# Cross-attention with layer norm: two key blocks evacuated ahead of a cast, the last eight pairs reordered

## The chip, the cores and the metric

The kernel runs on one core of a Trainium2 chip. The metric is the device time of one execution in microseconds (us), lower is better. The engines are TensorE (PE, its weight loads PEld), VectorE (DVE), ScalarE (ACT), GpSimd (POOL) and SyncE (SP, which only issues DMAs). Each engine works through its own instructions in program order.

## The reference

```python
# x (4, 2048, 512), context (4, 77, 512), mask (4, 2048, 77); 16 heads of 32; all float32
qs  = heads(x @ wq); ks = heads(ctx @ wk); vs = heads(ctx @ wv)
scores = einsum('bhqd,bhkd->bhqk', qs, ks) / sqrt(32)
scores = where(mask, -inf, scores)
attn   = einsum('bhqk,bhkd->bhqd', softmax(scores), vs)
out    = concat_heads(attn) @ wo + x
mu, var = mean(out), mean((out - mu)**2)          # over the 512 columns
result = (out - mu) / sqrt(var + 1e-5) * gamma + beta
```

## The kernel before

The 8192 rows are 64 tiles of 128 rows; two tiles make a block (32 blocks, called pairs), four tiles a group (16 groups, 512 rows). The context is so short that the keys (kct) and values (vsb) of all four batches stay in SBUF. Projections are done in split precision: an operand is cast to fp32r (the high part, by ScalarE) and the rest is kept as a low part (by GpSimd or VectorE), and three matmuls of 512 columns for each of 4 chunks, 12 in all, make one product.

The work is not scheduled by a compiler: the string ORDER lists it word by word, and each engine gets its part of the words in that order. A word is a letter with a number (a tile t, a pair b, or group times four plus part) and perhaps a part. The words used below:

- TensorE: S t scores of a tile (four PSUM banks sc, one for each place of a head in its group); Q one of four query projections of a group; V b product of probabilities and values of a pair (banks pa); W t the same for one tile, in the last pair; O t output projection (bank po); X t adds the residual x into po as a matmul by the identity, ahead of O t.
- VectorE: T t.n row maxima of four heads, with the mask (reads sc, writes pbuf); r reciprocal of the sums; t t transposes the probabilities (pbuf to B); q evacuates Q; b (and d in the last pair) the low part AL of the attention result; + residual into SBUF, $ residual in PSUM; s statistics (bn_stats, bn_aggr); y and z centring and finishing (subtract the mean and multiply by gamma; multiply by the inverse deviation and add beta).
- ScalarE: e t.n exponentials of four heads with their sums; a (c in the last pair) the high part AH of the attention result; i the cast of a half group of inputs (xth); k and % scale and shift a tile by its statistics; K evacuates a key block from PSUM into kct, in two instructions (J does so on VectorE).
- GpSimd: n normalises a tile's probabilities (h and m do so by halves for tile 63); j the low part of an input half (xtl); v, u, @ inverse deviations; f multiplies by gamma and adds beta.
- DMA: P b.n and U t.n move the transposed probabilities, in twelve pieces of a pair, from B to PT, on SyncE's queue (s), GpSimd's (g) or ScalarE's (a); x loads a tile for the residual, g a half group of inputs, w stores a tile.

A tile's path is S, T, e, r, n, t, P, V, a and b, O, then + or $, s, and either k with f, % with f, or y with z, then w. In the steady middle each pair of tiles repeats the same order of words. The last eight pairs (tiles 48 to 63) are written out in an order of their own, and in them the statistics are taken tile by tile.

Which of its buffers a tile takes is set by the strings SLOTS: "mm" gives the PSUM bank (0 to 7) for each product in the order of the program. A product waits until the reader of its bank's former holder is done. PADS gives the number of NO_OPs that stand between the matmuls of each projection. At the start, the words around the change are:

```python
... K2 A2 H2 J3 p i3 g4 J1 K0 i2 S0 I2 j2 S1 T0.1 ...
"K": lambda k, part: keys_evac(k, nc.scalar), "J": lambda k, part: keys_evac(k, nc.vector),
"i": lambda k, part: cast_xT(k // 2, k % 2 * 2),
```

H2 is a query projection of group 0, I2 its evacuation, S0 and S1 the first scores; i3 and i2 are the casts of group 1, whose inputs lie in stage_a.

Of the kernel before, what the change touches and what calls it, by code (L numbers as in the profile page):

```python
# [121 lines left out]
P24.3s M60.4 P25.11s T53.2 Q57 P25.4s e53.0 q58 P25.5s r52 T53.1 n52 P25.1s e53.2 b23.0 P25.2s T53.3 S54 P25.10s
e53.1 w43 v22 T54.0 Q56 e53.3 T54.1 x48 q57 P25.8s P25.3g q59 k42 P25.6s r53 T54.2 e54.1 n53 V24 b23.1 T54.3 e54.3
q56 x53 S55 f42 t52 a24.1 O46 a24.0 i31 t53 e54.2 b24.1 P26.10g P26.5s X49 i30 P26.6g +46 P25.7s P26.11g b24.0
P25.0s O49 P26.9a j31 T55.0 P25.9s e54.0 T55.3 P26.8s T55.1 w42 k45 T55.2 P26.1s j30 e55.0 S56 s46 r54 T56.1 O47
e55.3 T56.3 n54 s49 e55.2 T56.0 T56.2 S57 e56.0 f45 t54 V25 e55.1 T57.3 +47 O48 e56.2 w45 r55 P26.4g s47 P26.0s n55
a25.0 x55 T57.1 a25.1 P26.2s T57.2 e56.3 x57 Q61 $48 v23 t55 e56.1 u49 y49 P27.4s P26.7a Q63 b25.0 P26.3s e57.3
P27.11g q61 x51 P27.3g T57.0 P27.0s P27.1g e57.0 s48 P27.8g P27.2g r56 S58 b25.1 e57.2 P27.10g z49 n56 Q62 q63 k46
T58.2 k47 T58.1 e57.1 T58.3 f46 T58.0 V26 q62 e58.0 r57 t56 n57 S59 k44 w46 x61 e58.3 Q60 T59.0 P27.6s T59.1 P27.7s
e58.1 @48 T59.3 x50 t57 P27.9s f44 a26.1 P27.5s O50 a26.0 T59.2 e58.2 P28.8s q60 P28.9s b26.1 P28.5s e59.3 P28.6g  # L130
r58 b26.0 x63 S60 n58 $50 P28.3s e59.1 T60.1 O53 w44 T60.0 P28.1s %48 T60.2 x59 e59.2 P28.10g P28.0s t58 P28.2g
P28.11s X51 f47 e59.0 x56 T60.3 S61 +53 e60.0 T61.3 O51 r59 T61.2 n59 e60.1 T61.1 s50 e61.2 V27 T61.0 t59 P28.4g
e60.2 P28.7g f48 S62 s53 P29.8s e61.1 P29.2s T62.0 x58 s51 O52 a27.0 w47 a27.1 y51 w48 e60.3 P29.7g b27.0 P29.9s
u51 b27.1 P29.6s e61.3 y50 V28 P29.10s P29.1g r60 P29.0g z51 P29.11s e61.0 P29.3g T62.3 x54 n60 T62.2 x52 O55 a28.0
x62 T62.1 a28.1 r61 P29.5a b28.0 n61 b28.1 e62.1 t60 S63 e62.2 O57 t61 P29.4g e62.0 u50 T63.0 P30.2s @53 e62.3 +55
P30.6s O56 T63.2 P30.0s P30.5g T63.1 e63.0 P30.10s P30.11g r62 P30.3g s55 P30.8s n62 e63.1 P30.1s $52 X63 w51 T63.3
e63.3 V29 s52 @55 z50 e63.2 t62 @52 X62 P30.9a O54 h63.0 U62.5g U62.2s $56 a29.1 m63.0 a29.0 h63.1 U62.8s s56
P30.7a b29.0 m63.1 P30.4a b29.1 %52 O58 u56 t63 %55 f52 U62.4a $54 U62.3a U63.4s y56 U63.11s V30 $58 U63.0s z56
a30.0 U62.9s U63.10g s58 U62.11a U62.7s U63.7g O59 %53 $57 U62.1s U63.6g a30.1 U63.3g s57 U62.6s U62.10a @58 w52
b30.0 U63.1a U63.2s b30.1 u57 O61 U63.8a y57 f53 U63.5a s54 U62.0a z57 %58 y54 w57 U63.9a O60 $59 f55 +61 s61 s59  # L140
W62 @61 $60 w55 w53 s60 W63 u54 c62 w50 %61 u59 d62 O62 c63 u60 y59 z59 f61 d63 w59 z54 w56 y60 O63 z60 f58 w61 s62
w49 w54 y62 w60 s63 u62 w58 y63 u63 z62 z63 w62 w63
"""

SLOTS = {
    "mm": (
        "7012346570123576402317564023617520135647205130627431726352740136217364514036572140635170625341026713"
        "6427014536270652734107265320146735204167245310762435102367540123765427106345270163205417362045172463"
        "5071243650231764052371642750134627051320645731204657241360752431602357140623751427605341270653201467"
        "3520416724531076243510236754012376542710634527016320541736204517246350712465032634756320417537621047"  # L150
        "2362147310654130761370645732064023706457326475236123073042"
    ),
    "q": "1010101010101010",
    "xth": "010101010101010101",
# [4 lines left out]
    "AH": "1010010101010101010101010101010010",  # L159
    "AL": "1010010101010101010101010101010010",  # L160
    "o": "765401237654231607541237510462375104623751046237510462375104362",
# [17 lines left out]
def xattn_layernorm(  # L179
# [410 lines left out]
    def residual_psum(t):  # L590
        nc.vector.tensor_tensor(pos[t], pos[t], od[t], ALU.add)
# [36 lines left out]
    def moments_one(t):  # L628
# [3 lines left out]
        nc.vector.bn_aggr(mvs[t, 1][:, :2], st)
# [13 lines left out]

    def centre(t):
        o = pos.get(t, od[t])
        nc.vector.scalar_tensor_tensor(o, o, mvs[t, 1][:, 0:1], gam, ALU.subtract, ALU.mult)

    def finish(t):
        nc.vector.scalar_tensor_tensor(od[t], pos.pop(t, od[t]), mvs[t, 1][:, 2:3], bet, ALU.mult, ALU.add)
# [160 lines left out]
```

## Time and profile before

| what | value |
|---|---|
| median of 3 runs | 512.13 us (511.66 to 512.14) |
| the profiled execution's own time | 512.37 us |
| its span, first to last instruction | 510.5 us |
| mean granted TensorE clock | 0.997 |
| instructions in the span | 21819 |
| bytes moved by DMA | 110.95 MB, mean 217 GB/s |

A row of a stretch (A:B) gives its length, then for each engine the busy time with the number of instructions, the granted clock, the busy share of the DMA engines and GB/s. A row of the timeline gives the start, the time taken, engine, line, operation, output<-input and shapes; in brackets stands how long the engine was idle before it and what ended the wait. A row of the chain that ended last gives start, duration, engine, what was made and how many instructions were merged. A row of a group gives the count, the busy time and the mean in ns, then the idle time before. The times of the profile are those of one execution. Matmuls overlap, so the spacing of their starts says more than their listed length.

### The profile page before, as it was taken

The page shows a single profiled execution, that of the slowest core. Times are in us where ns is not written, and L with a number is a line of the kernel's source. Part 1 is how long each engine was busy: PE and PEld are TensorE (multiplying, and loading weights), DVE is VectorE, ACT ScalarE, POOL GpSimd, SP SyncE. Part 2 cuts the span into 40 slices and gives each one's busy share as a digit, 9 for nine tenths or more (in the row PEclk, how much of TensorE's full clock was granted, in tenths as well). Part 3 has the DMA queues.
Part 4 walks back from the last instruction along what each step waited for, and adds up shares of the span by engine and source line. Part 5 has one row for each costly group of instructions (what it writes and reads, how often), then busy time and mean ns, then how long its engine had stood idle before and what let it go on. Part 6 is the DMA issues. An engine that isn't in the chain of part 4 may idle for free.

```text
span 510.5 us, 21819 instructions
## 1 busy us (share of the span) xinstructions
PE 499.6 (98%) x6836; PEld 384.9 (75%) x6836; DVE 470.8 (92%) x2565; ACT 463.4 (91%) x2221; POOL 421.9 (83%) x389
## 2 busy tenths in 40 slices
PE   9999999999999999999999999999999999999994
PEld 7887777777777777777777877777777767776673
DVE  6698999999999999999999999999999899999897
ACT  6599999998999999999999999999999999899720
POOL 3473756899978998989899898888999689999896
PEclk9999999999999999999999999999999999999998
DMA  8947678868877777796768676876777875688655
GB/s 312 390 131 220 170 190 191 248 174 243 248 213 229 217 234 198 223 241 201 236 194 239 199 217 187 245 230 182 216 209 224 233 204 167 178 241 258 175 170 217
DMA packets 59139, 110.95 MB, mean 217 GB/s; under 512 B 9414, under 2 KB 11934, under 8 KB 59030
## 3 DMA queue, kind: packets, MB, share of 16 engines
q1 hardware_dynamic: 55094, 102.09, 68.7%
q0 software_dynamic: 2512, 5.84, 4.1%
q10 hardware_dynamic: 1424, 1.64, 1.2%
q8 instruction: 60, 0.98, 0.9%
q14 instruction: 49, 0.40, 0.3%
HBM read 41.79 MB, written 16.78 MB: 115 GB/s over the span
## 4 chain that ended last, share of the span: by engine, by line
PE 81%; POOL 7%; DMA 5%; DVE 4%; issue 1%; SPq 1%; ACT 0%; DVEq 0%; POOLq 0%; ACTq 0%
PE pq L290 33%; PE po L579 26%; PE sc L414 10%; PE pa L507 9%; DVE B L482 2%; PE pv L341 2%; DMA PT<-B 2%; DMA stage_a<-xT 2%; DMA stage_a<-wk 1%; POOL PT L493 1%; POOL o L621 1%; POOL xtl L273 1%; POOL pbuf L461 1%; POOL o L622 1%; POOL mvt L637 1%
## 5 line engine op out<-in xcount | busy, mean ns | idle before, releaser
L446 ACT ACTIVATE pbuf<-pbuf,nm 128x77 f32<-128x77 f32 x1024 | 352.4, 350 | 4.3 <-DVE nm L431 3.9
L446 ACT ACTIVATION_READ_ACCUMULATOR pbuf<-pbuf,nm 128x1 f32 x1024 | 195.5, 191 | 0.0
L431 DVE CUSTOM_DVE_ANT_0 pbuf<-sc,mb 128x77 f32<-128x77 f32 x1024 | 171.3, 233 | 9.1 <-PE sc L414 5.3
L461 POOL TENSOR_TENSOR pbuf<-pbuf,ri 128x1232 f32<-128x1232 f32 x63 | 142.8, 2267 | 30.4 <-DVE ri L456 28.9
L579 PE MATMUL po<-woh,AH 128*128 128x512 f32 x256 | 102.2, 399 | 1.8 <-DVE nm L431 1.4
L290 PE MATMUL pq<-xth,wqh 128*128 128x512 f32 (+1 forms) x256 | 101.3, 396 | 0.4
L579 PE MATMUL po<-woh,AL 128*128 128x512 f32 x256 | 100.0, 391 | 0.2
L579 PE MATMUL po<-wol,AH 128*128 128x512 f32 x256 | 99.8, 390 | 0.0
L482 DVE STREAM_TRANSPOSE B<-pbuf 128x1280 f32<-128x1280 f32 x64 | 95.9, 1500 | 2.9 <-POOL pbuf L473 1.4
L290 PE MATMUL pq<-xtl,wqh 128*128 128x512 f32 (+1 forms) x256 | 98.1, 383 | 0.0
L290 PE MATMUL pq<-xth,wql 128*128 128x512 f32 (+1 forms) x256 | 98.1, 383 | 0.0
L431 DVE DVE_READ_ACCUMULATOR2_ANT nm<- 128x1 f32 x1024 | 84.5, 83 | 0.0
L273 POOL TENSOR_TENSOR xtl<-xtf,xth 128x1024 fp32r<-128x1024 f32 x28 | 67.3, 2408 | 5.8 <-ACT xth L269 5.7
L622 POOL TENSOR_TENSOR o<-o,bet 128x512 f32<-128x512 f32 x52 | 67.3, 1294 | 4.1
L414 PEld LDWEIGHTS sc<-kct,q 32*64 32x64 f32 x4096 | 51.3, 130 | 23.7 <-issue 9.7
L621 POOL TENSOR_TENSOR o<-o,gam 128x512 f32<-128x512 f32 x52 | 68.4, 1315 | 0.2 <-issue 0.2
L414 PE MATMUL sc<-kct,q 32*64 32x77 f32 x4096 | 60.7, 238 | 0.9 <-ACT kct L326 0.9
L507 PE MATMUL pa<-PT,vsb 96*32 96x256 f32 x992 | 59.7, 382 | 0.0
L579 PEld LDWEIGHTS po<-woh,AH 128*128 128x128 f32 x256 | 48.1, 188 | 14.8 <-PE pa L507 1.0
L290 PEld LDWEIGHTS pq<-xth,wqh 128*128 128x128 f32 x256 | 48.0, 188 | 12.5 <-issue 1.2
L579 PEld LDWEIGHTS po<-woh,AL 128*128 128x128 f32 x256 | 48.0, 188 | 11.5 <-DVE AL L540 1.4
L579 PEld LDWEIGHTS po<-wol,AH 128*128 128x128 f32 x256 | 48.1, 188 | 9.8 <-issue 0.5
(120 smaller groups left out, 640.8 us busy)
## 6 DMA issues: line engine op xcount, KB each, us to landing
PT<-B SPq DMA_DIRECT2D x339, 128.0 KB
xtf<-xT SPq DMA_DIRECT2D x28, 512.0 KB
o<-x SPq DMA_DIRECT2D x56, 256.0 KB
out<-o SPq DMA_DIRECT2D x56, 256.0 KB
PT<-B POOLq DMA_DIRECT2D x26, 128.0 KB, 4.4
stage_a<-wk SPq DMA_DIRECT2D x4, 256.0 KB
stage_b<-wo SPq DMA_DIRECT2D x4, 256.0 KB
stage_a<-xT SPq DMA_DIRECT2D x2, 512.0 KB
```

What stands on the lines that cost most here:

```text
L273: nc.gpsimd.tensor_tensor(l[:, c : c + 2], fx.pop((g, c)), xh[g][:, c : c + 2].bitcast(F32), ALU.subtract)
L290: nc.tensor.matmul(pq, w[:, c, m * P : (m + 1) * P], r[g][:, c, rs], start=(n == 0), stop=(n == 11))
L341: nc.tensor.matmul(pv[: rows.stop - rows.start], ctx_s[c][i][:, rows], v[c], start=(n == 0), stop=(n == 11))
L414: mm = nc.tensor.matmul(sc[j][r0 : r0 + SR, g * NK : (g + 1) * NK], qs[q, g, rs.start + r0 : rs.start + r0 + SR], kct[q, g, t // TPB, keys ...
L431: nc.vector.tensor_tensor_reduce(pb[:, h // 2, (h % 2) * NK : (h % 2 + 1) * NK], scs[t][j][:, g * NK : (g + 1) * NK], mb[:, t % TPB, keys_ ...
L446: nc.scalar.activation(pb[:, h // 2, (h % 2) * NK : (h % 2 + 1) * NK], pb[:, h // 2, (h % 2) * NK : (h % 2 + 1) * NK], AF.Exp, bias=nmax[t ...
L461: nc.gpsimd.tensor_tensor(pv, pv, rv.to_broadcast((P, NP, 2, NK)), ALU.mult)
L482: nc.vector.transpose(bt.rearrange("p c q r -> p q c r"), pbuf[t % NPB].rearrange("p q (c r) -> p q c r", c=5),)
L507: nc.tensor.matmul(pas[b, g // 2][HD * j : HD * (j + 1), (g % 2) * BLK : (g % 2 + 1) * BLK], vsb[:, 2 * b // TPB, h % 2, HD * (h // 2) : H ...
L579: nc.tensor.matmul(pos[t], a[:, c, rs], w[:, c, :], start=(first and c == 0 and n == 0), stop=(c == NC_D - 1 and n == 2),)
L621: nc.gpsimd.tensor_tensor(o, o, gam, ALU.mult)
L622: nc.gpsimd.tensor_tensor(o, o, bet, ALU.add)
```

## The change

1. At the start, K0 is put ahead of the cast i3 (K0 g4 J1 i3 i2 in place of i3 g4 J1 K0 i2).
2. From g27 on, the input loads stand about a pair earlier; the order of the last eight pairs is new, with the PSUM banks that belong to it. The residual of tile 49 is added by VectorE ($49) in place of TensorE (X49); tile 48 is centred and finished by VectorE (u48 y48 z48) in place of ScalarE and GpSimd (@48 %48 f48); for 52 and 58 the residual goes to SBUF (+52, +58) in place of PSUM.
3. For tiles 60 and 62 ScalarE takes the statistics (=60, =62): one pass that sums the tile to minus its mean, and one that sums the squares of the centred values. GpSimd then scales that sum in place of adding epsilon alone.
4. Tile 63 is finished and stored in two halves of 256 columns (>63.0 <63.0 >63.1 <63.1), the first stored by SyncE's queue, the second by ScalarE's.
5. PADS is shifted at a few projections early in the program and around tile 26; there are 1466 NO_OPs in place of 1469. Some of the transposed pieces change their queue.

```diff
-... K2 A2 H2 J3 p i3 g4 J1 K0 i2 S0 I2 j2 S1 T0.1
+... K2 A2 H2 J3 p K0 g4 J1 i3 i2 S0 I2 j2 S1 T0.1
...
-    "i86800000000000000000686c10000cfmmlllllllllmmmmmmmmmmmmmmmmmmkkkkkkkkkkkkkkkkkkkkkkkkkkkkkkkkkjkkk00"
+    "f8680000000000000000000686000cddlmmllllllllmmmmmmmmmmmmmmmmmmmmikkkkkkkkkkkkkkkkkkkkkkkkkkkkkkjkkk00"
...
+    def stats_act(t):
+        mv = mvs[t, 1] = tiny.tile([P, 4], F32, tag="mvt", bufs=64 - LATE, name=f"mvt_{t}")
+        nc.scalar.activation(od[t], pos[t], AF.Copy, scale=-1.0 / D, accum_out=mv[:, 3:4])
+        nc.scalar.activation(od[t], pos[t], AF.Square, bias=mv[:, 3:4], accum_out=mv[:, 1:2])
+        by_act.add(t)
+
     def rsqrt_one(t):
         mv = mvs[t, 1]
-        nc.gpsimd.tensor_tensor(mv[:, 2:3], mv[:, 1:2], eps[:, :1], ALU.add)
+        if t in by_act:
+            nc.gpsimd.tensor_scalar(mv[:, 2:3], mv[:, 1:2], 1.0 / D, EPS, ALU.mult, ALU.add)
+        else:
+            nc.gpsimd.tensor_tensor(mv[:, 2:3], mv[:, 1:2], eps[:, :1], ALU.add)
         nc.gpsimd.tensor_tensor(mv[:, 2:3], mv[:, 2:3], mhalf[:, :1], ALU.pow)
...
     def centre(t):
         o = pos.get(t, od[t])
-        nc.vector.scalar_tensor_tensor(o, o, mvs[t, 1][:, 0:1], gam, ALU.subtract, ALU.mult)
+        m, op = (3, ALU.add) if t in by_act else (0, ALU.subtract)
+        nc.vector.scalar_tensor_tensor(o, o, mvs[t, 1][:, m : m + 1], gam, op, ALU.mult)
...
+    def finish_half(t, i):
+        cols = slice(i * D // 2, (i + 1) * D // 2)
+        nc.vector.scalar_tensor_tensor(
+            od[t][:, cols], pos[t][:, cols], mvs[t, 1][:, 2:3], bet[:, cols], ALU.mult, ALU.add
+        )
+
+    def store_half(t, i):
+        cols = slice(i * D // 2, (i + 1) * D // 2)
+        (nc.sync, nc.scalar)[i].dma_start(out[t * P : (t + 1) * P, cols], od[t][:, cols])
...
+        "=": lambda k, part: stats_act(k), ">": finish_half, "<": store_half,
```

TensorE's words from the scores of tile 52 on, before and after:

```
before: S52 V23 S53 Q59 Q58 Q57 S54 Q56 V24 S55 O46 X49 O49 S56 O47 S57 V25 O48 Q61 Q63 S58 Q62 V26 S59 Q60 O50
        S60 O53 X51 S61 O51 V27 S62 O52 V28 O55 S63 O57 O56 X63 V29 X62 O54 O58 V30 O59 O61 O60 W62 W63 O62 O63
after:  S52 V23 S53 Q56 Q58 S54 O46 Q59 S55 Q57 V24 S56 O47 O49 V25 S57 O48 Q60 Q61 S58 Q63 Q62 S59 V26 O50
        S60 X51 O53 S61 O51 S62 V27 O52 V28 O55 S63 O54 X63 O57 X62 V29 O56 O58 V30 O59 O61 O60 W62 W63 O62 O63
```

More of the change, by code (lines that the diff above doesn't have):

```diff
@@ L109 @@
 T44.0 e44.1 P20.1s T44.2 x40 S45 s36 a19.0 P20.0s e43.1 T44.3 Q48 v18 P20.3s t42 P20.9s P20.11s f34 k37 P20.8s
-T45.0 a19.1 P20.5s Q49 e44.2 T45.2 x43 r43 b19.1 n43 e44.3 b19.0 T45.3 T45.1 O39 e44.0 M48.4 f37 q49 e45.0 t43 O38
-e45.3 q48 P21.7s r44 w34 +39 i26 n44 P21.2s s39 k36 P21.4s S46 +38 e45.2 w37 V20 j26 T46.1 P21.10s T46.0 P21.6s
+T45.0 a19.1 P20.5s Q49 e44.2 T45.2 g27 r43 b19.1 x43 n43 e44.3 b19.0 T45.3 T45.1 O39 e44.0 M48.4 f37 q49 e45.0 t43
+O38 e45.3 q48 P21.7s r44 w34 +39 i26 n44 P21.2s s39 k36 P21.4s S46 +38 e45.2 w37 V20 j26 T46.1 P21.10s T46.0 P21.6s
@@ L122 @@
[L122 to L141, printed above, removed]
@@ L142 @@
-w49 w54 y62 w60 s63 u62 w58 y63 u63 z62 z63 w62 w63
+T51.2 P23.5s r49 g30 b22.1 x49 n49 e50.3 b22.0 T51.3 T51.1 O45 e50.0 q55 f43 t49 e51.0 q54 P24.7s O44 e51.3 r50 w40
++45 n50 P24.4s s45 e51.2 P24.3s P24.9s S52 i29 +44 x63 P24.2g M60.4 P24.11s V23 e51.1 T52.2 P24.1g P24.5s j29 T52.0
+P24.6s e52.2 T52.3 S53 P24.0s t50 x51 e52.3 Q56 P24.8s r51 T52.1 n51 a23.0 T53.0 e52.1 s44 Q58 q56 a23.1 v22 e52.0
+T53.2 b23.0 b23.1 P24.10a t51 S54 k44 e53.0 O46 r52 P25.3g P25.7s T54.1 n52 g31 T53.3 e53.2 P25.6s T53.1 w43 T54.0
@@ new lines @@
+e53.1 Q59 P25.2s T54.3 f44 x60 T54.2 e53.3 P25.11s t52 P25.5s e54.0 P25.9s S55 M56.4 P25.1s r53 +46 Q57 n53 e54.1
+q59 P25.10s T55.0 P25.0s e54.3 T55.2 P25.8s q58 P25.4g V24 e54.2 q57 t53 a24.0 S56 i30 T55.1 P26.10g P26.2s r54
+a24.1 O47 x56 T56.0 j30 e55.2 x57 b24.0 x48 b24.1 P26.0s e55.0 s46 P26.5s T55.3 O49 P26.11g w44 e55.3 T56.3 P26.4g
+P26.3s +47 n54 P26.8s T56.2 e55.1 P26.1s T56.1 V25 $49 e56.0 r55 t54 n55 e56.2 S57 x52 s49 O48 x58 i31 T57.3 u49
+y49 k42 j31 s47 e56.3 T57.0 Q60 T57.2 e57.3 f42 t55 a25.0 P26.7a z49 P27.7s Q61 e56.1 $48 w42 q60 P26.6g w49 T57.1
@@ new lines @@
+e57.2 P27.11g P26.9s s48 P27.1g S58 P27.3g e57.0 q61 x53 P27.2g y48 Q63 P27.4s u48 r56 a25.1 T58.2 n56 k45 T58.3
+e57.1 b25.0 T58.0 Q62 T58.1 e58.0 P27.8g z48 P27.10g r57 w48 b25.1 e58.1 n57 t56 P27.5s S59 P27.6s e58.2 V26 q62
+f45 T59.2 e58.3 t57 O50 a26.0 a26.1 T59.1 P28.11s e59.2 P27.0g T59.0 P28.1s P28.7g q63 P27.9s e59.0 v23 r58 S60
+b26.0 P28.9s T59.3 P28.8s X51 e59.1 n58 b26.1 P28.5s T60.1 O53 x59 T60.0 e59.3 P28.3s T60.2 P28.0s t58 e60.2
+P28.10g x55 P28.2g x61 S61 P28.4g e60.1 +53 P28.6g O51 r59 T60.3 n59 k47 T61.2 e60.3 T61.0 T61.3 f47 S62 T61.1
@@ new lines @@
+e60.0 t59 V27 e61.1 r60 T62.2 e61.3 P29.11s P29.0g T62.3 O52 P29.7g x50 s51 P29.4g P29.8s a27.0 T62.0 P29.3g a27.1
+P29.2s s53 P29.6g e61.0 w45 P29.1g V28 b27.0 P29.10s n60 y51 e61.2 x62 b27.1 T62.1 O55 a28.0 r61 @53 a28.1 $50
+e62.3 +52 n61 b28.1 b28.0 k46 S63 t60 e62.2 x54 f46 O54 e62.1 t61 P29.5a +55 w46 e62.0 T63.1 X63 P30.11g P29.9s
+T63.0 P30.5g O57 P30.6s P30.3g T63.2 e63.1 P30.1s u51 r62 s52 P30.0s n62 e63.2 s50 P30.2s P30.8s X62 T63.3 e63.3
+P30.10s s55 V29 u50 w47 y50 e63.0 @52 z51 @55 z50 w51 O56 a29.0 h63.0 P30.4a $57 m63.0 h63.1 a29.1 b29.0 P30.9a s57
@@ new lines @@
+m63.1 P30.7a b29.1 O58 %55 u57 t62 %53 f55 %52 $56 U62.2s U62.11a V30 $54 U62.1s U62.10a +58 U62.6s U62.3a f53 t63
+U62.4a O59 a30.0 a30.1 s58 U63.4s U63.1a U63.11s b30.0 @58 U62.8a U62.9s b30.1 U62.0a s56 U62.7s O61 U63.9a U62.5g
+y57 U63.10g U63.3a s54 U63.6g U63.0s U63.5a U63.7g U63.2s y54 U63.8a u54 w50 O60 +61 %58 f52 w53 z54 s61 $59 y56
+W62 @61 s59 W63 c62 u56 z57 u59 c63 d62 O62 $60 f58 y59 =60 d63 z59 %61 y60 O63 w59 u60 =62 z56 w58 f61 z60 w57 y62
+w56 w60 s63 w52 w55 u62 y63 w61 u63 z62 w54 w62 >63.0 <63.0 >63.1 <63.1
@@ L158 @@
     "B": "0101011010101010101010101010101010",
[L159 to L161 removed]
+    "AH": "1010010101010101010101010101010101",
+    "AL": "1010010101010101010101010101010101",
+    "o": "765401237654231607541237510462375104623751046237510462375160714",
     "nm": "0120102101201201201201201201201201201201201201201201201201201201",
@@ L259, in xattn_layernorm @@
     od, pos, mvs, rns, vd, ris, parts = {}, {}, {}, {}, {}, {}, {}
-    ends, tmps, xs = {}, {}, {}
+    ends, tmps, xs, by_act = {}, {}, {}, set()
     pe_words = [w for w in ORDER.split() if w[0] in "HBQSVWXO"]
```

21 lines of the change are left out of this document (9 added, 12 removed).

## The prediction

> **What bounds the kernel now.** I read the page first, then busy time by stretches, then the chain that ended last, and then the timeline at the two ends where the change stands. The page:
>
> ```profile
> PE 499.6 (98%) x6836; PEld 384.9 (75%) x6836; DVE 470.8 (92%) x2565; ACT 463.4 (91%) x2221; POOL 421.9 (83%) x389
> PE 81%; POOL 7%; DMA 5%; DVE 4%; issue 1%; SPq 1%; ACT 0%; DVEq 0%; POOLq 0%; ACTq 0%
> ```
>
> TensorE is busy 98% of the span and carries 81% of the chain that ended last. The stretches (length, then busy time of PE, PEld, DVE, ACT, POOL, then the granted clock) show where that stops being true:
>
> ```profile
> 300.00:400.00 100.00, 100.00 (x1443) 77.64 (x1442) 93.73 (x532) 97.43 (x473) 89.07 (x73) 1.00 0.75 213
> 388.00:413.00 25.00, 25.00 (x335) 19.22 (x336) 22.85 (x141) 24.65 (x133) 19.41 (x16) 1.00 0.87 235
> 413.85:476.01 62.16, 60.70 (x883) 44.75 (x865) 60.62 (x351) 60.19 (x310) 57.30 (x63) 1.00 0.72 203
> 500.00:510.50 10.50, 3.81 (x17) 2.82 (x15) 7.06 (x12) 0.00 (x0) 5.87 (x8) 0.86 0.59 227
> ```
>
> In the steady middle TensorE has no gap and the others have slack. From 414 to 476, the last pairs, four engines are within 8% of full: VectorE has only 1.5 us idle in 62. So a gain there needs TensorE and VectorE to be relieved together. After 503.8 TensorE is done and VectorE with the last stores is left. The waits of TensorE and of its neighbours, in total:
>
> ```profile
> PE po L579 <- DVE nm L431: 1.4, 2, 0.9
> PE sc L414 <- ACT kct L326: 0.9, 1, 0.9
> ```
>
> The second is the start, the first two are projections of the last pairs that wait for a PSUM bank which VectorE's row maxima have not yet freed.
>
> **The change, part by part. The start.** ScalarE's queue here holds the key blocks (kct) and the input casts of group 1 (xth from stage_a). Before:
>
> ```order
> L326 ACTIVATE kct<-pk_228 128x4x77
> L326 ACTIVATE kct<-pk_228 128x4x19
> L269 CAST xth_334<-stage_a 128x1024
> L326 ACTIVATE kct<-pk_226 128x4x77
> L326 ACTIVATE kct<-pk_226 128x4x19
> L269 CAST xth_334<-stage_a 128x1024
> ```
>
> After:
>
> ```order
> L326 ACTIVATE kct<-pk_228 128x4x77
> L326 ACTIVATE kct<-pk_228 128x4x19
> L326 ACTIVATE kct<-pk_226 128x4x77
> L326 ACTIVATE kct<-pk_226 128x4x19
> L269 CAST xth_340<-stage_a 128x1024 x2
> ```
>
> The second key block no longer stands behind a cast. What that cast waits for, on the timeline of ScalarE and TensorE:
>
> ```profile
> 17.40 0.55 ACT L326 ACTIVATE kct<-pk 128x308 f32<-128x308 f32 x2 [3.06 <-PE pk L313]
> 20.17 1.05 ACT L269 CAST xth<-stage_a 128x1024 fp32r<-128x1024 f32 x1 [2.21 <-DMA stage_a<-xT]
> 20.37 0.28 PE L290 MATMUL pq<-xth,wql 128*128 128x256 f32 x1
> 21.12 0.54 ACT L326 ACTIVATE kct<-pk 128x308 f32<-128x308 f32 x2
> 21.55 1.04 ACT L269 CAST xth<-stage_a 128x1024 fp32r<-128x1024 f32 x1
> 21.60 1.80 PE L414 MATMUL sc<-kct,q 32*64 32x77 f32 x128 [0.94 <-ACT kct L326]
> 22.94 0.36 ACT L446 ACTIVATE pbuf<-pbuf,nm 128x77 f32<-128x77 f32 x1 [0.34 <-DVE nm L431]
> ```
>
> The block will be done at about 18.5, inside ScalarE's idle 2.21, so the first scores start when TensorE ends its projections (20.65): a gain of 0.94. The two casts move up by only 0.43 (21.55 to 21.12). If ScalarE's exponentials set the pace of the next stage the gain is 0.43; since TensorE is the engine without gaps afterwards I take 0.9. Range 0.4 to 0.95.
>
> **The last eight pairs on TensorE.** Its rows in the chain that ended last:
>
> ```profile
> 395.94 0.88 PE sc L414 x52
> 396.82 1.86 PE pa L507 x32
> 418.97 4.76 POOL xtl L273 x2
> 431.47 5.44 PE pq L290 x24
> 446.39 2.72 PE po L579 x12
> 449.99 2.92 PE po L579 x12
> 452.91 0.86 PE po L566 x2
> 473.39 3.99 DMA PT<-B
> ```
>
> and its last matmul with what VectorE does behind it:
>
> ```profile
> 503.43 0.39 PE L579 MATMUL po<-woh,AL 128*128 128x512 f32 x1
> 503.63 0.76 DVE L649 SCALAR_TENSOR_TENSOR po<-po,mvt,gam 128x512 f32<-128x512 f32 x1
> 504.30 0.69 DVE L630 BATCH_NORM_STATS2 st<-po 128x6 f32<-128x512 f32 x1
> 505.24 0.76 DVE L649 SCALAR_TENSOR_TENSOR po<-po,mvt,gam 128x512 f32<-128x512 f32 x1
> 505.91 1.40 DVE L652 SCALAR_TENSOR_TENSOR xtl<-po,mvt,bet 128x512 f32<-128x512 f32 x2
> 506.68 0.99 SPq L625 DMA_DIRECT2D out<-xtl  x2
> ```
>
> From the scores of tile 52 to the end of projection 63 TensorE takes 503.8 - 395.9 = 107.9 us. Its work there: 12 scores at 0.88 (10.6), 8 value products at 1.86 (14.9), two half ones (at most 1.9), 26 projections at 2.72 (70.7), 0.20 more for each of the 15 that follow scores or values (2.92 against 2.72; 3.0), 4 residual matmuls at 0.86 (3.4): 104.5, so 3.4 us are waits. The new order has the same kinds, the same 15 switches, and one residual matmul less (X49 becomes $49 on VectorE): 103.6. The most that the tail can give is 107.9 - 103.6 = 4.3.
>
> What it gives is less, because VectorE stands close behind. Ahead of the last maxima of tile 63 it does in addition $49, y48, z48, +52 and s52, and leaves y50, z51, s55 and $52 for later. With these rows
>
> ```profile
> L649 DVE SCALAR_TENSOR_TENSOR po<-po,mvt,gam 128x512 f32<-128x512 f32 x10 | 7.5, 749 | 0.1
> L652 DVE SCALAR_TENSOR_TENSOR o<-po,mvt,bet 128x512 f32<-128x512 f32 x4 | 2.9, 714 | 0.0
> L591 DVE TENSOR_TENSOR po<-po,o 128x512 f32<-128x512 f32 x4 | 2.7, 682 | 0.4 <-PE po L579 0.4
> L630 DVE BATCH_NORM_STATS2 st<-po 128x6 f32<-128x512 f32 x13 | 9.0, 692 | 0.1
> L632 DVE BATCH_NORM_AGGREGATE mvt<-st 128x2 f32<-128x6 f32 x16 | 2.9, 182 | 0.5
> L645 ACT ACTIVATE o<-po,mvt 128x512 f32<-128x512 f32 x2 | 1.5, 768 | 0.2 <-issue 0.2
> L446 ACT ACTIVATION_READ_ACCUMULATOR pbuf<-pbuf,nm 128x1 f32 x233 | 44.4, 191 | 0.0
> L622 POOL TENSOR_TENSOR o<-o,bet 128x512 f32<-128x512 f32 x11 | 14.2, 1288 | 0.9
> ```
>
> the added work is 0.68 + 0.75 + 0.71 + 0.68 + 0.87 = 3.7, the removed 0.75 + 0.71 + 0.87 + 0.68 = 3.0: 0.7 more. Against that the new order brings scores 54 to 56 and 62 ahead of some projections (a value product now stands between scores 62 and projection 52, where TensorE waited 0.9), so VectorE's idle time can close: 1.5 between 414 and 476, and of the 2.15 before it (388 to 413) I take a third, 0.7. The tail gains 1.5 + 0.7 - 0.7, about 1.5; bounds -1 to 4.3.
>
> Edits at nothing: GpSimd loses f48 (twice 1.29, 2.6 us) and one small operation, and wins slack. Of 24 last transposed pieces ScalarE now issues 11 in place of 9; they stand ahead of its casts c62 and c63, which wait for the same pieces anyway. The loads g27 to g31 go out a pair earlier and find their buffer free. The fewer NO_OPs sit behind matmuls. One cover is thin: cast i31 now stands eight groups of four exponentials (4 x 0.35 each) and one cast (1.05) later on ScalarE, 12.2 us. GpSimd's two splits end at 423.7 now (418.97 + 4.76), 7.7 ahead of the projections at 431.5; one of them is off that path and saves 2.4, so some 12.2 - 2.4 - 7.7 = 2.1 is not covered but for the 1.4 that the first half of a projection takes: 0 to 1 us of wait, inside the bounds above.
>
> **The end.** VectorE's queue (mvt holds a tile's mean and variance) before:
>
> ```order
> L652 SCALAR_TENSOR_TENSOR xtl_15_8868<-po_60_10422,mvt_60_10472,bet_77 128x512
> L630 BN_STATS st_62_10541<-po_62_10262 128x6
> L632 BN_AGGR mvt_62_10543<-st_62_10541 128x2
> L649 SCALAR_TENSOR_TENSOR po_62_10262<-po_62_10262,mvt_62_10543,gam_76 128x512
> L630 BN_STATS st_63_10549<-po_63_10216 128x6
> ```
>
> After:
>
> ```order
> L662 SCALAR_TENSOR_TENSOR xtl_15_8749<-po_60_10413,mvt_60_10505,bet_77 128x512
> L659 SCALAR_TENSOR_TENSOR po_62_10208<-po_62_10208,mvt_62_10527,gam_76 128x512
> L630 BN_STATS st_63_10539<-po_63_10153 128x6
> L632 BN_AGGR mvt_63_10541<-st_63_10539 128x2
> L659 SCALAR_TENSOR_TENSOR po_63_10153<-po_63_10153,mvt_63_10541,gam_76 128x512
> L662 SCALAR_TENSOR_TENSOR xtl_15_8749<-po_62_10208,mvt_62_10527,bet_77 128x512
> L666 SCALAR_TENSOR_TENSOR xtl_15_8749<-po_63_10153,mvt_63_10541,bet_77 128x256 x2
> ```
>
> Statistics 62 are gone from in front of centring 62. That centring ran from 503.63, past the last matmul, and held statistics 63 until 504.30; they can now start at 503.9: 0.4 gained. ScalarE pays two passes from PSUM, 2 x (0.77 + 0.19) = 1.9 a tile, while projection 63 (2.7) runs. The trace has no 256-wide finish and no half store. Each half costs at least half of 0.71 and at most all of it: 0 to 0.7 more in all; a half store saves at most half of its issue-to-end time. I take 0 for the two together, range -0.5 to +0.5. The Trainium skill (VectorE: DVE Perf Modes, section on the TRN2 errata) gives a VectorE instruction that reads PSUM a fixed 120 cycles, so the second half would add an estimated 0.13 us; by it the sum would be 0.1 smaller. It also says (DMA: Bandwidth & Descriptors, Anatomy of one DMA) that some 2.0 us of a transfer do not scale with its size, which speaks against halving; by it a half store saves an estimated 0.3 us. No row here separates either.
>
> **Sum.** 0.9 + 1.5 + 0.4 = 2.8 from the profiled run's 512.37 (span 510.5 and 1.9 around it) is 509.6; the median of the runs is 0.24 lower, so 509.3.
>
> **Rivals.** *TensorE and VectorE both close up*: 0.95 + 4.3 + 0.6 = 5.8 gives 506.3. For it: the waits are on banks that the order changes; against: VectorE's 1.5 us. *VectorE paces the tail*: none of its idle time closes, so the 0.7 is added and X49's 0.86 frees nothing: 0.9 - 0.7 + 0.4 = 0.6, 511.5, no change. *Slower, by GpSimd's store in SyncE's queue*. SyncE's queue at the pieces PT_29 before, with stores 47 and 48:
>
> ```order
> L625 DMA out<-o_47_8237 128x512
> L625 DMA out<-o_48_9022 128x512
> L493 DMA PT_29_9963<-B_29_9792 32x2x512 x4
> L548 DMA o_54_10050<-x 128x512
> L548 DMA o_52_10057<-x 128x512
> ```
>
> After:
>
> ```order
> L625 DMA out<-o_7890 128x512
> L493 DMA PT_9962<-B_9789 32x2x512
> L548 DMA xtl_8749<-x 128x512
> L548 DMA o_10119<-x 128x512
> L625 DMA out<-o_8480 128x512
> L493 DMA PT_9962<-B_9789 32x2x512
> L493 DMA PT_10155<-B_10113 32x2x512 x6
> ```
>
> Store 46 (o_8480) now stands ahead of a piece of PT_29 and all six of PT_30. It waits for affine 46, which GpSimd does after normalising tile 61:
>
> ```profile
> 467.53 2.26 POOL L461 TENSOR_TENSOR pbuf<-pbuf,ri 128x1232 f32<-128x1232 f32 x1 [0.38 <-DVE ri L456]
> 476.43 0.42 PE L507 MATMUL pa<-PT,vsb 96*32 96x256 f32 x4
> ```
>
> At the pace of before that is 469.8 + 2.6 = 472.4, then store and piece (about 1) and 4.0 to land: 477.4, 1.0 after the place of value product 29 now (476.43). If GpSimd is 3 us later still, the tail loses 4.0 and keeps 0.9 + 0.4 from the ends: 2.7 slower, 514.8; it decides from affine 46 ending later than about 472.7 on the time scale of before. Against it: GpSimd has 2.6 us less to do and idled 4.9 of the 62 us. *That the change does not do what it says*, an activation table loaded for the new ScalarE functions, is not in the program's order.
>
> **How the numbers follow.** Forecast (507.5 to 511.0) 0.63, both close up 0.08, VectorE paces 0.11, slower 0.18. A run of this kernel can tell some 0.2% from no change, so faster is below 511.1: 0.71; same 0.11; slower 0.18. The range leaves out a little of the best case and the slower rival: 506.8 to 513.0.
>
> **What would show it.** Right: the first scores at about 20.7 with no wait on kct; the last matmul at about 501.3; statistics 63 directly behind it; no residual matmul for tile 49. Wrong: a TensorE wait of over 1 us at the projections 60 to 63 of the last input group or at value product 29 or 30, or TensorE's last matmul no earlier than 503.

## The result, and the profile after

| kernel | median of its runs | profiled execution | span |
|---|---|---|---|
| before | 512.19 us (511.66 to 512.40, 6 runs) | 512.37 us | 510.5 us |
| changed | 510.09 us (509.67 to 510.68, 6 runs) | 509.93 us | 508.1 us |

The ratio is 0.9961, 95% interval 0.9948 to 0.9974: 2.0 us faster, where 2.8 were forecast. Measured once more, beside other runs of the kernel before, the changed kernel stood at 0.995 (0.9933 to 0.9968), 2.6 us faster.

Busy time and the shares of the chain that ended last, from the page of the changed kernel:

```profile
PE 497.6 (98%) x6834; PEld 384.0 (76%) x6834; DVE 471.3 (93%) x2565; ACT 465.6 (92%) x2228; POOL 420.0 (83%) x388
PE 85%; DVE 5%; DMA 4%; POOL 3%; SPq 2%; issue 1%; ACTq 0%; ACT 0%; DVEq 0%
```

TensorE has 2.0 us less to do and four points more of the chain; GpSimd's share is down from 7% to 3%. The stretches of the last pairs and of the end, and TensorE's waits in total:

```profile
386.00:411.00 25.00, 25.00 (x334) 19.54 (x340) 23.95 (x152) 25.00 (x132) 20.92 (x18) 1.00 0.75 211
411.40:473.60 62.20, 61.84 (x888) 45.28 (x876) 61.72 (x355) 61.14 (x317) 55.13 (x60) 1.00 0.75 208
498.00:508.10 10.10, 3.20 (x15) 2.31 (x13) 6.31 (x11) 2.06 (x6) 5.66 (x9) 0.89 0.75 286
```

```profile
PE po L579 <- DVE AL L540: 0.8, 1, 0.8
PE pa L522 <- DVE po L591: 0.5, 1, 0.5
PE po L579 <- DVE nm L431: 0.4, 1, 0.4
```

VectorE's idle time from 411 to 474 is 0.5 (1.5 before), and 1.05 in the stretch ahead of it (2.15 before). The waits for banks that the row maxima free (1.4 before) are down to 0.4, but two waits are new, both in the last pair. The start, on ScalarE and TensorE:

```profile
7.23 0.40 ACT L251 CAST xth<-first_xth 128x256 fp32r<-128x256 f32 x1 [1.45 <-DMA first_xth<-xw]
...
17.70 1.00 ACT L326 ACTIVATE kct<-pk 128x308 f32<-128x308 f32 x4 [2.87 <-PE pk L313]
...
19.51 1.99 ACT L269 CAST xth<-stage_a 128x1024 fp32r<-128x1024 f32 x2 [0.81 <-DMA stage_a<-xT]
...
20.88 1.75 PE L414 MATMUL sc<-kct,q 32*64 32x77 f32 x128
```

The key block no longer stands behind the cast, and the first scores wait for nothing. But two arrivals differ from the run shown of before, and no edit stands ahead of either: the third piece of the first weights is there at 7.23 (6.73 before), the first input of group 1 at 19.51 (20.17). The last pair and the end, on TensorE, VectorE and ScalarE's queue:

```profile
491.01 0.75 DVE L662 SCALAR_TENSOR_TENSOR o<-po,mvt,bet 128x512 f32<-128x512 f32 x1 [1.07 <-POOL mvt L646]
...
491.86 1.08 PE L522 MATMUL pa<-PT,vsb 96*32 96x128 f32 x32
...
495.19 0.68 DVE L540 TENSOR_TENSOR AL<-pa,AH 128x512 fp32r<-128x512 f32 x1
...
495.92 0.50 PE L579 MATMUL po<-woh,AL 128*128 128x512 f32 x1 [0.78 <-DVE AL L540]
...
500.81 0.39 PE L579 MATMUL po<-woh,AL 128*128 128x512 f32 x1
...
501.19 1.26 POOL L622 TENSOR_TENSOR xtl<-xtl,bet 128x512 f32<-128x512 f32 x1
501.24 0.70 DVE L630 BATCH_NORM_STATS2 st<-po 128x6 f32<-128x512 f32 x1
...
502.19 0.76 DVE L659 SCALAR_TENSOR_TENSOR po<-po,mvt,gam 128x512 f32<-128x512 f32 x1
...
503.40 0.75 DVE L662 SCALAR_TENSOR_TENSOR xtl<-po,mvt,bet 128x512 f32<-128x512 f32 x1 [0.46 <-POOL mvt L646]
...
504.19 0.87 DVE L666 SCALAR_TENSOR_TENSOR xtl<-po,mvt,bet 128x256 f32<-128x256 f32 x2
...
505.10 0.36 ACTq L672 DMA_DIRECT2D out<-xtl  x1
```

The last matmul ends at 501.20, 2.6 before its time in the kernel before. Projection 62 waits in its third matmul for the low part d62, and the finish of tile 62 waits 0.46 for GpSimd, which is busy with the affine of tile 61 until 502.45.

The whole comparison fits into a table of stretches, read from the timeline of each run's profile. A: start of the first scores; B: from there to the scores of tile 52; C: from there to the end of the last matmul; D: from there to the end of the span (the span is given to 0.1, so D is good to 0.05). The arrivals at the start put A up to 1.4 apart between kernels with the same instructions ahead of it, so a part is judged by B, C and D as well as by the time. "Ratio" is to the kernel before on the same chip, with its 95% interval.

| kernel | A | B | C | D | median us | ratio |
|---|---|---|---|---|---|---|
| before | 21.60 | 374.27 | 107.94 | 6.69 | 512.19 | 1 |
| changed | 20.88 | 374.10 | 106.22 | 6.90 | 510.09 | 0.9961 (0.9948 to 0.9974) |
| changed, again | 20.32 | 374.92 | 106.20 | 6.96 | 510.15 | 0.9950 (0.9933 to 0.9968) |
| start alone | 21.64 | 374.50 | 107.99 | 6.67 | 512.25 | 0.9991 (0.9977 to 1.0004) |
| without the start | 21.09 | 374.37 | 106.27 | 6.97 | 510.51 | 0.9959 (0.9946 to 0.9971) |
| whole last store | 21.68 | 374.09 | 106.38 | 7.15 | 510.72 | 0.9958 (0.9946 to 0.9970) |
| statistics on VectorE | 21.17 | 374.29 | 106.30 | 7.84 | 511.26 | 0.9966 (0.9954 to 0.9978) |
| d62 early | 20.84 | 374.24 | 105.48 | 8.04 | 510.37 | 0.9953 (0.9936 to 0.9970) |
| residual 49 on TensorE | 20.34 | 376.07 | 107.18 | 6.91 | 511.59 | 0.9973 (0.9960 to 0.9985) |
| affine 61 split | 20.24 | 374.58 | 106.24 | 7.24 | 510.55 | 0.9957 (0.9941 to 0.9974) |
| stores by completion | 20.25 | 375.25 | 106.19 | 6.91 | 510.19 | 0.9959 (0.9943 to 0.9976) |
| F0 later | 21.51 | 375.05 | 106.24 | 6.90 | 509.97 | 0.9958 (0.9944 to 0.9972) |
| stores, split, residual 59 | 20.81 | 374.62 | 106.10 | 7.27 | 510.22 | 0.9957 (0.9944 to 0.9970) |
| tail retimed | 21.34 | 374.33 | 106.27 | 6.96 | 510.33 | 0.9958 (0.9941 to 0.9974) |

### The profile page after: what moved, and what is told of

The parts are those of the page before. It is cut to its first block, busy times and chain, and to the rows that moved or that the text cites. A ratio compares the mean times of both kernels' runs of the same rounds, so it can differ in the third digit from the quotient of the medians.

```text
span 508.1 us, 21810 instructions
## 1 busy us (share of the span) xinstructions
PE 497.6 (98%) x6834; PEld 384.0 (76%) x6834; DVE 471.3 (93%) x2565; ACT 465.6 (92%) x2228; POOL 420.0 (83%) x388
## 4 chain that ended last, share of the span: by engine, by line
PE 85%; DVE 5%; DMA 4%; POOL 3%; SPq 2%; issue 1%; ACTq 0%; ACT 0%; DVEq 0%
PE pq L290 33%; PE po L579 28%; PE sc L414 10%; PE pa L507 10%; PE pv L341 2%; DVE pbuf L431 1%; DVE B L482 1%; PE pk L313 1%; DMA xtl<-x 1%; DMA PT<-B 1%; SPq L493 1%; DMA first_xth<-xw 1%; POOL mvt L646 1%; PE pq L724 1%; DVE q L304 0%
## 5 line engine op out<-in xcount | busy, mean ns | idle before, releaser
L622 POOL TENSOR_TENSOR o<-o,bet 128x512 f32<-128x512 f32 x51 | 66.0, 1294 | 4.0
L621 POOL TENSOR_TENSOR o<-o,gam 128x512 f32<-128x512 f32 x51 | 67.0, 1314 | 0.2 <-issue 0.2
L290 PEld LDWEIGHTS pq<-xth,wql 128*128 128x128 f32 x256 | 48.1, 188 | 9.7
```

The lines of the kernel that those rows point to most:

```text
L290: nc.tensor.matmul(pq, w[:, c, m * P : (m + 1) * P], r[g][:, c, rs], start=(n == 0), stop=(n == 11))
L621: nc.gpsimd.tensor_tensor(o, o, gam, ALU.mult)
L622: nc.gpsimd.tensor_tensor(o, o, bet, ALU.add)
```

## The experiments

**The start, done alone and undone.** The first kernel is that before with

```diff
-... H2 J3 p i3 g4 J1 K0 i2 S0
+... H2 J3 p K0 g4 J1 i3 i2 S0
```

the second is the changed kernel with the same line turned back.

> The kernel before with the start's edit alone (second key block ahead of the first input cast on ScalarE). Theory (TensorE sets the pace from the first scores on): the first scores start about 0.9 us earlier than the 21.60 of before and all of it is carried to the end: 511.3, i.e. 0.9 below before. Rival A (ScalarE's exponentials set the pace of the next stage): only the 0.43 by which the casts move arrives, 511.8. Rival B (the last pairs are paced by another engine, which does not start earlier): nothing arrives, 512.2.

> The changed kernel with the start's edit undone (the first cast again between the two key blocks). Theory: the first scores come 0.9 us later, the new tail keeps what it gives: 510.1 + 0.9 = 511.0. Rival A: 0.4 later, 510.5. Rival B (the new tail is paced by VectorE and had swallowed the start's gain): 510.1.

Alone it was worth 0.0009 of the time, 0.5 us (-0.2 to 1.2); with it undone the changed kernel kept a ratio of 0.9959, within 0.5 us of its own two. Both values lie under the 0.9 of the theory and near the 0.4 of rival A, but the interval of the first holds 0, 0.4 and 0.9 alike: the times alone decide nothing. The traces do. First that without the edit:

```profile
19.67 1.05 ACT L269 CAST xth<-stage_a 128x1024 fp32r<-128x1024 f32 x1 [1.99 <-DMA stage_a<-xT]
...
20.62 0.55 ACT L326 ACTIVATE kct<-pk 128x308 f32<-128x308 f32 x2
...
21.09 1.17 PE L414 MATMUL sc<-kct,q 32*64 32x77 f32 x72 [0.72 <-ACT kct L326]
```

Here the scores start 1.42 after the cast (1.43 in the run of before). With the edit they start when TensorE is free. The other end of the stage is in the second profile of the changed kernel, where the scores started at 20.32.

**The changed kernel again.**

> The changed kernel once more, as the measure for the three beside it and for the start. First scores in the runs so far: 21.60 and 21.09 with the old order of the key blocks (a wait of 0.95 and 0.72 in front), 20.88, 21.64, 21.68 and 21.17 with the new one (no wait). Theory A (the arrival of the very first weights differs from run to run by more than the wait that the edit removes, and the edit itself is worth 0 to 0.9): this run's first scores lie anywhere from 20.6 to 21.7, without a wait. Rival (the edit itself brings the first weights later): not before 20.8, and the projection of the first block waits 0.5 to 0.9 for its weights again. Time 509.7 to 510.8.

```profile
19.68 2.00 ACT L269 CAST xth<-stage_a 128x1024 fp32r<-128x1024 f32 x2 [1.54 <-DMA stage_a<-xT]
...
21.76 4.75 POOL L273 TENSOR_TENSOR xtl<-stage_a,xth 128x1024 fp32r<-128x1024 f32 x2 [3.31 <-ACT xth L269]
...
25.71 1.35 DVE L370 TENSOR_TENSOR wvlAH<-stage_b,wvh 128x512 fp32r<-128x512 f32 x1
...
28.36 0.70 PE L414 MATMUL sc<-kct,q 32*64 32x77 f32 x38 [0.33 <-DVE q L306]
```

The third piece of the first weights was there at 6.21 and no projection waited for it, so the rival falls: the late weights of the runs before were chance. Scores 0 came early, and scores 2 then waited 0.33 for VectorE's copy of q. VectorE was late because its split of a weight (F0, line 370) took 1.35: it ended at 27.06, 0.55 after GpSimd's two splits of the input, which can begin only when ScalarE has done both casts. In the first profile of the changed kernel the same two stand like this:

```profile
21.59 4.75 POOL L273 TENSOR_TENSOR xtl<-stage_a,xth 128x1024 fp32r<-128x1024 f32 x2 [2.58 <-ACT xth L269]
...
26.27 0.69 DVE L370 TENSOR_TENSOR wvlAH<-stage_b,wvh 128x512 fp32r<-128x512 f32 x1
```

There F0 begins as GpSimd ends and takes 0.69. Two rules of timing hold through all runs. With the new order the scores of tile 2 start either 7.60 to 7.62 after those of tile 0 (six runs, two of them with F0 later, below), or 8.67 to 8.69 after the first cast (the other six: start alone, changed again, residual 49, affine 61 split, stores, stores with split). With the old order they start 9.15 after the first cast (two runs of two). So the edit is worth 9.15 - 8.68 = 0.47 at the most, and less where the first weights, not the input of group 1, come late: in the profile of the changed kernel 19.51 + 9.15 - 28.50 = 0.16. The Trainium skill (SBUF — State Buffer, section on the two separate sides) says that a VectorE operation with two inputs from SBUF and a GpSimd operation that reads SBUF hold a port pair for themselves in turn, the other blocking. F0 has two such inputs, and the trace agrees in that F0 ends behind GpSimd's split; a wait for all of that split and 0.69 of work behind it would put 0.69 between the two ends, and 0.55 were measured.

The two engines meet again some 5 us later, at the next split of a weight (F2) and GpSimd's split j5, and the fourteen profiles hold both orders of arrival. In the six runs of the second rule GpSimd starts 0.3 ahead and takes 2.40, and F2 takes 2.62 to 2.64 and ends 0.55 after it. In the other eight F2 starts 0.08 ahead and takes 0.69, and GpSimd's split takes 2.86 to 2.89. So each delays the other, whichever comes second.

**F0 behind the copy of q.**

```diff
-... e0.3 F0 T1.3 I0 e1.2 r0 n0 S2 ...
+... e0.3 T1.3 I0 F0 e1.2 r0 n0 S2 ...
```

> The changed kernel with VectorE's weight split F0 behind, not ahead of, the last maxima of tile 1 and the copy of q (I0) that the scores of tile 2 read. In the runs where the scores of tile 0 began at 20.2 to 20.3 this split took 1.35 to 1.47 instead of 0.69 and ended 0.5 after GpSimd's two splits, and the scores of tile 2 began 8.04 to 8.16 after those of tile 0 instead of 7.62. Theory A (the split may not read SBUF while GpSimd's split does, so the start's gain is given back there, and GpSimd starts only when ScalarE has done both input casts): scores 2 now start 7.6 after scores 0, also if scores 0 start before 20.5, without a wait for the copy of q; up to 0.45 earlier in such runs, 0 in others. Rival B (VectorE is late for another reason, its maxima or its waits for PSUM): scores 2 still 8.0 to 8.2 behind when scores 0 start early. The time: 509.7 to 510.2.

F0 took 0.68 and scores 2 came 7.60 behind scores 0, but these began at 21.51, late, and then the theory asks for 7.6 anyway. The run tells nothing apart; the last kernel has the same edit, and its first scores were late as well (21.34). That GpSimd's split holds F0 rests on the two rules and on F2's two orders of arrival, not on an intervention; that it is the port is what the skill says, and no run here isolates it.

**The residual of tile 49 back on TensorE.**

```diff
-... e55.0 s46 P26.5s T55.3 O49 ... V25 $49 e56.0
+... e55.0 s46 P26.5s T55.3 X49 O49 ... V25 e56.0
```

> The changed kernel with the residual of tile 49 back on TensorE (one matmul of 0.86) instead of on VectorE (0.68). Theory A (TensorE sets the pace of the tail, as the sum had it): 0.9 later, 511.0, and from the scores of tile 52 to the last matmul 107.1 instead of 106.2. Rival B (VectorE sets it): 0 to 0.7 earlier, 509.4 to 510.1. Rival C (each has as much slack as the other takes): no change.

C grew by 0.98 to 107.18: theory A. TensorE paces these pairs, and its residual matmul counts in full. The time grew by 1.4 against the changed kernel beside it, more than the 0.9 of the theory; its profiled execution also has one wait of 0.92 at 72.9, far ahead of the edit, which makes B longer.

**d62 ahead of VectorE's other work.**

```diff
-... y56 W62 @61 s59 W63 c62 u56 z57 u59 c63 d62 O62 $60 f58 y59 =60 d63 z59
+... y56 W62 @61 W63 c62 d62 s59 u56 z57 u59 c63 O62 $60 d63 f58 y59 =60 z59
```

> The changed kernel with the low halves d62 and d63 ahead of statistics 59 and of centring 59 on VectorE, so that projection 62 finds its third operand in time. Theory A (TensorE's idle before and in projections 62 is an order of VectorE that could be had otherwise, but VectorE is full by then): the last matmul ends 1.0 to 1.4 earlier (from the first scores of tile 52 on: 105.0 instead of 106.2), the end gains 0 to 0.5: 509.6 to 510.1. Rival B (TensorE sets the end): all of it arrives, 508.9. Rival C (the statistics that were moved back make centring 59 and GpSimd's scale of 59 late): slower, 510.6.

```profile
493.82 1.08 PE L522 MATMUL pa<-PT,vsb 96*32 96x128 f32 x32 [0.59 <-DVE po L591]
...
501.39 0.69 DVE L630 BATCH_NORM_STATS2 st<-po 128x6 f32<-128x512 f32 x1
```

The wait for d62 is gone, that of value product 63 for $59 stays, and the last matmul ends 0.72 earlier in C, at 500.56. But statistics 63 begin at 501.39, since VectorE is still busy with what was put back, and D grows by 1.1. The time is the same (510.37 against 510.15). That is theory A in kind, with less than the 1.0 to 1.4 that it asked of the last matmul. Counted from the scores of tile 52, VectorE's last finish ends at 110.15, against 110.05 in the changed kernel beside it: from tile 59 on VectorE has no room, and TensorE's waits in the last pair cost nothing. Of D's 1.1, 0.7 are the earlier matmul, 0.1 is this finish, and 0.25 are that the end of the span comes 3.33 after it in place of 3.08; whether the stores still queued do that, no run tests.

**The statistics of 60 and 62 back on VectorE**: s60 and s62 in place of =60 and =62.

> The changed kernel with the statistics of tiles 60 and 62 back on VectorE (0.88 us each) at the same places of the order. Theory (only statistics 62 stood on the path, and half of it): 0.4 later, 510.5. Rival A (VectorE has no slack left from statistics 59 to the end): both count, 1.7 later, 511.8. Rival B (GpSimd's affine of tile 61 holds the scale of tile 62 anyway, so VectorE's wait of 0.46 before the finish of 62 takes up the statistics): 510.1.

D is 7.84, 0.9 longer, and C the same: more than the theory's 0.4, less than the 1.7 of rival A. The ratio (0.9966) is too near that of the changed kernel to show it; the trace is one execution. Of the 0.9, 0.6 are VectorE's last finish, which comes later, and the rest is a longer way from there to the end of the span (3.47 against 3.08), again not explained. VectorE had no room left:

```profile
501.72 0.74 DVE L662 SCALAR_TENSOR_TENSOR xtl<-po,mvt,bet 128x512 f32<-128x512 f32 x1
502.38 0.75 DVE L659 SCALAR_TENSOR_TENSOR po<-po,mvt,gam 128x512 f32<-128x512 f32 x1
503.04 0.69 DVE L630 BATCH_NORM_STATS2 st<-po 128x6 f32<-128x512 f32 x1
```

The last matmul of this kernel ended at 501.76, and two operations stand between it and statistics 63.

**The last store whole**: z63 and w63 in place of the halves.

> The changed kernel with the last finish and store of tile 63 undivided (one finish of 512, one store on SyncE). Theory (halving is worth nothing, since the second half store leaves about as late as a whole one would): 510.1, within 0.2. Rival (the smaller last transfer lands earlier): 510.4 to 510.6. Rival the other way (two finishes cost 0.87 against 0.75 and a second issue): 509.9.

D is 7.15, 0.2 longer: the edge of the theory's 0.2, and less than the 0.3 to 0.5 of the first rival, whose direction it has. The ratio does not show it. Its finishes of 62 and 63 end at 505.87 and the span 3.43 later; with halves it is 3.08. The two half finishes take 0.87 where a whole one takes 0.75.

**GpSimd's affine of 61 in two.**

```diff
-... z56 w58 f61 z60 w57 y62 w56 w60 s63 w52 w55 u62 y63 w61 u63 z62 w54 w62 >63.0 <63.0 >63.1 <63.1
+... z56 w58 [61 z60 w57 y62 w56 w60 s63 w52 w55 u62 y63 u63 ]61 z62 w54 w62 >63.0 <63.0 w61 >63.1 <63.1
```

([ multiplies by gamma, ] adds beta.)

> The changed kernel with GpSimd's affine of tile 61 taken apart: its second half (1.3 us) behind the scales of tiles 62 and 63, store 61 behind the first half store. Theory A (the 0.46 that VectorE waits ahead of the finish of 62 is GpSimd's affine, and it is on the path): the wait goes, 0.5 earlier, 509.6; from the last matmul to the end 6.4 instead of 6.9. Rival B (store 61 is now the one that lands last, or delays a half store in SyncE's queue): 0 or 0.3 later.

```profile
502.88 1.26 POOL L772 TENSOR_TENSOR xtl<-xtl,bet 128x512 f32<-128x512 f32 x1
503.38 0.87 DVE L666 SCALAR_TENSOR_TENSOR xtl<-po,mvt,bet 128x256 f32<-128x256 f32 x2
...
504.39 0.40 SPq L625 DMA_DIRECT2D out<-xtl  x1
```

The first half of theory A came true, and rival B decided. The wait went, and VectorE finished 3.2 after the last matmul (3.9 in the changed kernel); but store 61 is issued at 504.39, is now the last to land, and D is 7.24, 0.3 longer.

**The stores in the order of completion.** In the changed kernel SyncE's queue holds store 59 at its head:

```profile
SPq L625 <- DVE xth L662: 9.5, 1, 9.5
```

This edit puts the finished tiles ahead of it:

```diff
-... z54 s61 ... O63 w59 u60 =62 z56 w58 f61 z60 w57 y62 w56 w60 s63 w52 w55 u62 y63 w61 u63 z62 w54 w62 ...
+... z54 w55 w54 s61 ... w52 z57 w57 ... z59 w59 ... w58 z56 w56 f61 z60 w60 y62 s63 u62 y63 w61 u63 z62 w62 ...
```

> The changed kernel with the last stores in the order in which their tiles are done (55, 54, 52, 57, 59, 58, 56, 60, 61, 62, 63) instead of with store 59 in front. In the changed kernel SyncE waits 9.5 us for tile 59 with four finished tiles behind it, and the DMA engines then move some 400 GB/s without a gap from 498.4 to 506. Theory A (the end is bound by the DMA engines, which is why the statistics that left VectorE gained nothing there): from the last matmul to the end 6.3 to 6.7 instead of 6.9, the time 0.2 to 0.6 lower, 509.5 to 509.9 against 510.1. Rival B (VectorE's last finish and the fixed landing of a store bound the end): no change in that stretch, 510.1.

What the DMA engines moved from 480 to 512, in 40 slices, first in the changed kernel, then in this one:

```profile
GB/s 343 100 138 199 202 35 124 208 199 202 204 326 199 275 282 31 0 0 20 0 0 0 0 0 376 410 407 399 402 407 407 407 374 26 0 0 0 10 0 0
```

```profile
GB/s 384 67 0 195 204 176 0 183 208 206 201 201 361 170 318 391 333 133 128 220 79 243 5 0 131 410 376 269 126 97 230 49 385 232 0 0 10 0 0 0
```

The gapless stretch at 400 GB/s is broken up, and D is what it was, 6.91. My theory fell: the full queue is hidden, and the end is VectorE's last finish and some 3.1 for the last store.

**Two versions meant to beat both.** The first joins the stores and the split and moves residual 59 to TensorE (X59 ahead of O59, $59 gone). The second has F0 later, the stores, u54 ahead of two transposed pieces on GpSimd, $59 ahead of s61, and d62 and d63 early.

> A version meant to beat both: the stores in the order of completion; GpSimd's affine of tile 61 in two halves with the scales of tiles 62 and 63 between; the residual of tile 59 as a matmul on TensorE (0.86) instead of 0.68 on VectorE, ahead of d62. Theory A (with the DMA engines unloaded VectorE's chain sets the end): the last finish ends 0.66 earlier by the split and up to 0.68 by the residual, O62 waits less; 0.8 to 1.6 below the changed kernel, 508.5 to 509.3. Rival B (the residual costs TensorE its 0.86, and VectorE was not the bound): 0.2 to 0.6 below, 509.5 to 509.9. Rival C (store 61, now the last but one to be ready, is the end): no gain, 510.1.

> A version meant to beat both, from what the runs before showed: GpSimd's scale of tile 54 ahead of two of its transposed pieces (VectorE waited 1.07 for it before the finish of 54), residual 59 ahead of statistics 61 (the value product 63 waited for its PSUM bank), d62 and d63 ahead of other VectorE work, the stores in the order of completion, and at the start the weight split F0 behind the copy of q. Theory A (VectorE's chain from tile 54 to the last finish sets the end, with waits of 1.07, 0.38, 0.2 and 0.45 in it, the projection's waits being a consequence): from the scores of tile 52 to the last matmul 104.8 to 105.4 instead of 106.2, from there to the end 6.6 to 7.0, so 0.8 to 1.4 below the changed kernel, 508.7 to 509.3. Rival B (as with d62 alone, what TensorE gains is lost behind it: 0.7 earlier there, 1.1 more from the last matmul to the end): 510.1. Rival C (the pieces that were put back behind the scale of 54 reach the value product 63 late): it waits 0.3 to 0.8 for the pieces, 509.5 to 510.1. At the start: scores 2 come 7.6 after scores 0 if these begin before 20.5 (theory of GpSimd's split against VectorE's), 8.0 and more if another reason holds VectorE.

Neither did. In the first store 61 ends last again (D 7.27): rival C. Rival B holds too: from the scores of tile 52 the last finish comes at 109.35, 0.7 earlier than in the changed kernel, but the split alone had brought it to 109.42. Residual 59 off VectorE gained next to nothing, since VectorE then waits 0.77 in place of 0.19 ahead of the finish of tile 60 for GpSimd's inverse deviation. In the second the value product 63 waits for the pieces that were put back:

```profile
495.17 1.08 PE L522 MATMUL pa<-PT,vsb 96*32 96x128 f32 x32 [1.33 <-DMA PT<-B]
```

That is rival C too, with 1.33 where 0.3 to 0.8 were expected, and C is 106.27 again.

## Why the prediction was right, and where its terms were off

The direction and the range held: 2.0 us, and 2.6 when measured again, where 2.8 were forecast. Of the three terms of the sum one was near its size and two were not.

**The start, 0.9.** This step failed. It took TensorE as the engine that sets the pace and put aside the 0.43 by which the casts move. The measured bound is that one, 0.47, though not by the exponentials as the text supposed: the path goes from the second cast over GpSimd's split, VectorE's F0 and the copy of q to the scores of tile 2. The first scores at 20.88 and those of tile 52 at 394.98 (0.89 earlier) look like a hit; 0.66 of that is the input that arrived earlier in this run. The last matmul at 501.20, for which 501.3 was named, has the same luck in it.

**The tail, 1.5.** C fell by 1.7; the size was met partly by luck. The sum let VectorE limit the gain: 1.5 + 0.7 of its idle time closes, 0.7 of work is added, and the residual X49 that TensorE loses (0.86) adds nothing of its own. VectorE's idle time closed by 1.0 + 1.1, near what was put, and X49 came on top in full, 0.98 as measured. So VectorE was not the limit for most of the tail. What was not seen is the last pair. Value product 62 starts 96.9 after the scores of tile 52, in the kernel before

```profile
495.78 1.95 PE L522 MATMUL pa<-PT,vsb 96*32 96x128 f32 x64
```

99.9 after: by there the tail had gained 3.0, and it gave back 1.3 in the waits for $59 and d62, where VectorE was behind. This is rival two (VectorE paces) in the last ten microseconds alone. TensorE's listed waits in C are 1.8 before (the 1.4, and 0.4 for a bank that a finish frees) and 1.7 after: they moved to the last pair, and C fell by the residual and by smaller changes of spacing. The prediction had put 3.4 us of waits there, from a sum of durations; some 1.6 of them are no waits in the list, so the rival in which both engines close up (4.3 from the tail) had less to win than it said.

**The end, 0.4.** D grew by 0.2. Statistics 63 do begin 0.04 after the last matmul, 0.45 better than before, as worked out. The step left out that GpSimd's affine of tile 61 runs until 502.45 and holds the scale of tile 62: the finish of 62 waits 0.46 for it. Between the two profiles this makes -0.45 up to statistics 63, +0.54 from centring 63 to the finish of 62 (0.67 before, 1.21 after), +0.26 for the finishes of 62 and 63 (1.40, 1.66), and -0.14 from there to the end of the span (3.22, 3.08). The halving, taken at 0, is worth 0.2 against a whole store in the changed kernel: it costs VectorE 0.12 and lands some 0.35 sooner. Here the Trainium skill's estimates came near, 0.13 (VectorE: DVE Perf Modes, the TRN2 errata) and 0.3 (DMA: Bandwidth & Descriptors, Anatomy of one DMA, a section on DMAs that GpSimd issues; these stores go out by SyncE and ScalarE). ScalarE's statistics are worth 0.9, not 0.4: VectorE was full, and the way from its last finish to the end was 0.4 longer without them.

**The edits at nothing.** Cast i31 cost nothing (the projections of the last group start at 428.98 without a wait; 0 to 1 us was allowed). Affine 46 ended at 469.87, which is 470.8 on the time scale of before (0.89 later), ahead of the 472.7 from which the slower rival would decide, and no piece PT_29 was late.

## What to carry to other kernels

A wait in one profile is an upper bound for what its removal gives: look for the next input of the same stage, here a cast that stays where it was, and what it feeds on three other engines. Where two engines close up together, the gain of the one is handed over at the last step; it has to be summed to the last instruction of the other. Parts below the spread of the run times can still be told by stretches of the trace that start behind the noise.

## What the runs showed that I had not expected

The cast of the third piece of the first weights began between 6.21 and 8.04 in fourteen profiles, in twelve of them after a wait for the piece, with the same instructions ahead of it; the first scores lay up to 1.4 apart, and where it came at 7.2 or later they began 13.6 behind it. VectorE's two-input split took 0.69 beside an idle GpSimd, up to 1.95 (F0) and 2.64 (F2) beside a split of GpSimd's that had begun first. And ten stores and two halves of one that go out without a gap at 400 GB/s nearly to the end cost the changed kernel nothing that the other order of them could win back.
